# Graph attention on one Trainium2 core: the first stage's edge preparation moved between engines and places

## The chip, the cores and the metric

The kernel runs on one core of one Trainium2 chip. The metric is the device time of one execution in microseconds (us). Engines are called as in the profile: PE (TensorE matmul), PEld (its weight load), DVE (VectorE), ACT (ScalarE), POOL (GpSimd), SP (SyncE, which here only issues transfers).

## What is computed

There are 12,500 nodes with 128 features `x` and 212,500 directed edges, sorted by target `dst`, each with 128 features `edge_attr_128` and one weight. There are 8 heads of 16.

```python
h = relu(layernorm(x))
q = h @ Wq.T + bq ; v = h @ Wv.T + bv          # per node
k = edge_attr_128 @ Wk.T + bk                  # per edge
in_m   = sum(q[src] * k, -1)                   # per edge and head
out_m  = sum(q[dst] * k, -1)
diag_m = sum(q[src] * q[dst], -1)
score  = (segsoftmax(in_m / 4, dst) + segsoftmax(out_m / 4, dst)
          + segsoftmax(diag_m / 4, dst)) * edge_weight1 ** lam
agg = segment_sum(score * v[dst], dst)
out = x + leaky_relu(agg @ Wo.T + bo, 0.1)
```

## The kernel before

The path that runs (`ordered_path`) has a first stage over nodes and a loop over edges.

**First stage.** The nodes lie in 98 tiles of 128, in `xq`. They are loaded in nine parts: tiles 0-3, 4-7, 8-13, 14-27, 28-41, and so on to 84-97. Each part gets statistics on DVE (`statistics`: L817 per tile, then five small sums L822 to L827), and then its scale and shift (`scale`: a square root on ACT L832, a reciprocal L833 and a shift L834 on DVE). 25 groups of four tiles go through a pipeline written out by hand: in step g, ACT rectifies group g + 2 in place (L845), PE turns group g + 1 (L852) and ACT copies it (`hT`, L854), PE multiplies group g by Wq (L860), DVE adds the bias (L863), and SP stores the rows into `q_table` in memory (L864). Then come the scale of a part that is needed four groups on (`ready`), and the statistics of a later part (`measure`).

After that, the dictionary `side` may call a piece of edge preparation in step g. The edge arrays are loaded by POOL as 104 rows of 2048 (`src_r`, `dst_r`, `weight`):

- `edges_1` (step 2) makes the source indices float on DVE (L750) and turns them with 16 PE transposes (L734) and four DVE copies (L735) into `src_i`, the indices of the gathers.
- `edges_2` (step 8) makes the targets float on POOL (L754), subtracts neighbours on DVE (`step`, L756; it takes the buffer of `src_r`), and marks the starts of segments on POOL (L758), stored as term 0 of `fa_d`.
- `edges_3` (step 11) takes each block's base (L763) and subtracts it (L766, four times), on DVE; POOL reorders and casts the result (L769) for `rel_d`.
- `edges_4(c)` (steps 14, 17, 20) splits the weights into three bf16 terms: a POOL copy (L775), a DVE subtraction (L777), and a store of term c + 1 (L743).
- `turn_ws` and `biases` (steps 5, 6) prepare the other weights and biases.

The bf16 results of `edges_2`, `edges_3` and `edges_4` share two buffers (`of`).

After the last group, `gather(0..8)` is issued on POOL, then `fetch_edges(0..5)` (the edge features of six blocks of 512 edges, L644), `fetch(0)` on SP, and `terms_q` (L880 to L889), which splits q into three bf16 terms for `q3_table`.

**Edge loop.** 420 blocks of 512 edges. Each has four indirect gathers of q rows on POOL (L652), issued nine blocks ahead (`LOOK`), and the products, scans and row sums on PE, ACT and DVE.

**Order.** `pin` chains every instruction of an engine in program order. So each engine, SP's queue of transfers too, runs its list in the order of the code, and a waiting instruction holds all behind it.

Of the kernel before, what the change touches and what calls it, by code (L numbers as in the profile page):

```python
# [472 lines left out]
def ordered_path(ctx: ExitStack, tc: tile.TileContext, flag, x, src, dst, edge_attr, edge_weight,  # L473
# [19 lines left out]
    nc = tc.nc  # L493
# [12 lines left out]
    RC = RB * BE  # L506
# [14 lines left out]
    def parts_of(u):  # L521

        return [s for s in range(S)
                if (s == 0 or START * s + RATE - NEAR < UN * (u + 1))
                and (s == S - 1 or UN * u < START * (s + 1) + RATE + NEAR)]
# [59 lines left out]
    LOOK, QQ, AHEAD, EA = 9, 11, 6, 7  # L585
# [6 lines left out]
    def pin(inst):  # L592

        engine = str(inst.ins.engine)
        if engine in pinned:
            tc.add_manual_dep(inst.ins, pinned[engine], mybir.DependencyInfo(
                mybir.DependencyClass.NoSync, mybir.DependencyReason.DATA), reason="in order")
        pinned[engine] = inst.ins.name
        return inst
# [14 lines left out]
    def fetch(t):  # L614

        if t >= T:
            return
        at, part = block_rows(t)
        relb = load.tile([K3, S, BE], BF, name="relb")
        pin(nc.sync.dma_start(relb, rel_d[part].rearrange("(s b) e -> s b e", b=G)  # L620
                              [None, :, at, :].to_broadcast([K3, S, BE])))
        fa = load.tile([4 * S, BE], BF, name="fa", bufs=4)
        for s in range(S):
            pin(nc.sync.dma_start(fa[4 * s:4 * s + 4], fa_d[s * G + t]))
        _, base_v[t] = nc.values_load_multi_w_load_instructions(
            bases[0:1, t, 0:S], engines=[mybir.EngineType.SP], min_val=0, max_val=N - 1,
            skip_runtime_bounds_check_because="the indices of nodes are below N")
        st[t] = dict(relb=relb, fa=fa)
# [8 lines left out]
    def fetch_edges(g):  # L637
        if g < S * T:
            ea = load.tile([P, JN * F], F32, name="ea", bufs=EA)
            b0 = (g % S * G + g // S) * BE  # L640
            n = min(BE, E - b0)
            if n < BE:
                nc.vector.memset(ea, 0.0)
            pin(nc.sync.dma_start(ea[:n // JN, :],  # L644
                                  edge_attr[b0:b0 + n, :].rearrange("(p j) f -> p (j f)", j=JN)))
            eas[g] = ea

    def gather(g):
        if g < S * T:
            qq = gath.tile([P, JN, 2, F], F32, name="qq")  # L650
            for j in range(JN):
                rows = pin(nc.gpsimd.indirect_dma_start(  # L652
                    out=qq[:, j, 0, :], out_offset=None, in_=q_table,
                    in_offset=bass.IndirectOffsetOnAxis(
                        ap=src_i[:, g % S * G + g // S, j:j + 1], axis=0)))
                if (g - LOOK, j) in behind:
                    tc.add_manual_dep(rows.ins, behind[g - LOOK, j], mybir.DependencyInfo(
                        mybir.DependencyClass.Sync, mybir.DependencyReason.SCHED_ONLY),
                        reason="close behind the products")
            qqs[g] = qq  # L660
# [15 lines left out]
    with tc.tile_pool(name="prep", bufs=1) as prep, \  # L676
# [30 lines left out]
        src_r = prep.tile([RW, RC], I32, name="src_r", tag="step")  # L707
# [3 lines left out]
        dst_r = prep.tile([RW, RC + 2], I32, name="dst_r")  # L711
# [5 lines left out]
        weight = prep.tile([RW, RC], F32, name="weight")  # L717
# [11 lines left out]
        def turn_edges(of, to, which=range(RB)):  # L729
            cols = of.rearrange("r (a p j) -> r a j p", a=RB, j=JN)  # L730
            for a in which:
                t_ps = prep_ps.tile([P, JN, RW], F32, name="t_ps")
                for j in range(JN):
                    pin(nc.tensor.transpose(t_ps[:, j, :], cols[:, a, j, :], ident[:RW, :RW]))  # L734
                pin(nc.vector.tensor_copy(to[:, a:NB:RB, :], t_ps.rearrange("p j r -> p r j")))  # L735

        dst_f = dst_r.bitcast(F32)
        src_f = src_r.bitcast(F32)
# [3 lines left out]
        def fa_out(c, of):  # L742
            pin(nc.sync.dma_start(fa_d.rearrange("(r a) c e -> c r a e", a=RB)[c],  # L743
                                  of.rearrange("r (a e) -> r a e", a=RB)))

        def of_tile():
            return prep.tile([P, RC], BF, name="of", bufs=2)[:RW]

        def edges_1():
            pin(nc.vector.tensor_copy(src_f, src_r))  # L750
            turn_edges(src_f, src_i)

        def edges_2():
            pin(nc.gpsimd.tensor_copy(dst_f, dst_r))  # L754
            step = got["step"] = prep.tile([RW, RC + 1], F32, name="step", tag="step")
            pin(nc.vector.tensor_sub(step, dst_f[:, 1:], dst_f[:, :RC + 1]))  # L756
            of = of_tile()
            pin(nc.gpsimd.tensor_scalar(of, step[:, :RC], 0.0, -FAR, op0=ALU.is_gt, op1=ALU.mult))  # L758
            fa_out(0, of)
# [13 lines left out]
        def edges_4(c):  # L773
            of = of_tile()
            pin(nc.gpsimd.tensor_copy(of, weight))  # L775
            if c < 2:
                pin(nc.vector.tensor_sub(weight, weight, of))  # L777
            fa_out(c + 1, of)

        def edges_5(i):  # L780
# [11 lines left out]
        def turn_w(i, to):  # L792
            w_ps = prep_ps.tile([P, F], F32, name="t_ps")
            pin(nc.tensor.transpose(w_ps, w_in[:, i, :], ident))
            pin(nc.scalar.copy(to, w_ps))
# [47 lines left out]
        def rectify(g):  # L843
            for i in tiles_of(g):
                pin(nc.scalar.activation(xq[:, i, :], xq[:, i, :], AF.Relu, bias=shift[:, i:i + 1],  # L845
                                         scale=inv[:, i:i + 1]))

        def turn_h(g):
            n = len(tiles_of(g))
            h_ps = node_ps.tile([P, JN, P], F32, name="h_ps")  # L850
            for b, i in enumerate(tiles_of(g)):
                pin(nc.tensor.transpose(h_ps[:, b, :], xq[:, i, :], ident))  # L852
            hT = hTs[g] = node.tile([P, JN, P], F32, name="hT", bufs=2)
            pin(nc.scalar.copy(hT[:, :n], h_ps[:, :n]))  # L854

        def nodes_q(g):
            n = len(tiles_of(g))
            q_ps = node_ps.tile([P, JN, F], F32, name="q_ps")
            for b in range(n):
                pin(nc.tensor.matmul(q_ps[:, b, :], hTs[g][:, b, :], wq, start=(b == 0),  # L860
                                     stop=(b == n - 1)))
            q = xq[:, g * JN:g * JN + n, :]
            pin(nc.vector.tensor_add(q, q_ps[:, :n], bq_all[:, None, :].to_broadcast([P, n, F])))  # L863
            pin(nc.sync.dma_start(units(q_table, g * 2, n // 2, F),  # L864
                                  q.rearrange("p (u k) f -> p u (k f)", k=2)))
            del hTs[g]
# [3 lines left out]
        def terms_q(g):  # L870
# [11 lines left out]
            if g > 0:  # L882
# [7 lines left out]
                    q3_table[3 * lo:3 * (lo + n * P), :].rearrange("(u p k) f -> p u (k f)", p=P, k=6),  # L890
                    q3.rearrange("p (u k) t f -> p u (k t f)", k=2)))

        side = {2: edges_1, 5: turn_ws, 6: biases, 8: edges_2, 11: edges_3, 14: lambda: edges_4(0),
                17: lambda: edges_4(1), 20: lambda: edges_4(2)}
        turn_w(0, wq)
        parts = [(2 * lo, 2 * hi) for lo, hi in zip(LOADS, LOADS[1:])]

# [2 lines left out]
        def measure(upto):  # L900

            while parts and parts[0][0] < (upto + 1) * JN:
                measured.append(statistics(*parts.pop(0)))

        def ready(upto):

            while measured and measured[0][0] < (upto + 1) * JN:
                scale(*measured.pop(0))
# [3 lines left out]
        for g in range(-2, GN):  # L912
            if g + 2 < GN:
                rectify(g + 2)
            if 0 <= g + 1 < GN:
                turn_h(g + 1)
            if g >= 0:
                nodes_q(g)
            ready(g + 4)
            measure(g + 6 + min(max(g, 0), 6))  # L920
            if g in side:
                side[g]()
        for g in range(LOOK):
            gather(g)
        for g in range(AHEAD):
            fetch_edges(g)
        fetch(0)
        for g in range(GN + 1):
            terms_q(g)
# [142 lines left out]
    with tc.tile_pool(name="work", bufs=2) as work, \  # L1072
# [223 lines left out]
        for g in range(end + 2 * S):  # L1296
# [31 lines left out]
            if g < S:  # L1328
                of = [u for u in range(NU) if g in parts_of(u)]
# [62 lines left out]
```

## Time and profile before

| | |
|---|---|
| median of 3 runs | 2300.62 us (2298.96 to 2305.27) |
| profiled execution: own time, span | 2308.75 us, 2307.0 us |
| busy: PE, PEld, DVE, ACT, POOL | 1816.2, 1395.9, 2148.9, 1515.6, 1666.3 us |
| shares of the span | 79%, 61%, 93%, 66%, 72% |
| moved by DMA | 341.04 MB, 148 GB/s on average |
| mean granted TensorE clock | 0.79 |

The times of instructions come from one profiled execution, whose span starts with its first instruction. A row of the timeline gives the start, the duration, the engine and the line, then output and input with their shapes; "xN" merges N neighbours, and the bracket tells how long the engine had been idle and what released it. A group row gives the total busy time, the mean of one in ns, and the idle time before them. Durations on POOL are rough.

### The profile page before, as it was taken

What the parts mean: (1) busy time and instruction counts of PE and PEld (TensorE: products, weight loads), DVE (VectorE), ACT (ScalarE), POOL (GpSimd) and SP (SyncE); (2) the same over time, 40 slices, a digit from 0 to 9 for tenths busy, and PEclk for the clock granted to TensorE, in tenths of its full rate; (3) what the DMA queues carried; (4) which work ended last, traced back from release to release, by engine and by line L of the source; (5) the groups of instructions that cost most, each with busy time, mean ns of one, the idle gap of its engine ahead of it and who ended that gap; (6) DMA issues with size and microseconds to landing.
All of it is one profiled execution on the core that took longest, in us unless ns stands there. A gap on an engine that the chain in (4) does not pass through costs nothing.

```text
span 2307.0 us, 36031 instructions
## 1 busy us (share of the span) xinstructions
PE 1816.2 (79%) x10629; PEld 1395.9 (61%) x10629; DVE 2148.9 (93%) x2263; ACT 1515.6 (66%) x2797; POOL 1666.3 (72%) x1715
## 2 busy tenths in 40 slices
PE   5458888888878778888777887878788878778876
PEld 4446666666666566666566665666566666556654
DVE  6889999998999999999999999999999999999994
ACT  5667676666676666667666666657666667666772
POOL 3677777777777777777777777777777777777760
PEclk8767777776787797888788778878787788788786
DMA  7785455455454545555544555455555545544531
GB/s 198 242 262 146 144 142 151 135 155 139 129 157 138 149 140 142 154 147 140 156 134 146 145 147 158 136 144 142 152 145 142 153 143 142 158 140 141 142 97 41
DMA packets 306681, 341.04 MB, mean 148 GB/s; under 512 B 137667, under 2 KB 225496, under 8 KB 306165
## 3 DMA queue, kind: packets, MB, share of 16 engines
q1 hardware_dynamic: 244042, 222.69, 32.1%
q0 software_dynamic: 54448, 112.96, 19.3%
q10 hardware_dynamic: 7984, 3.00, 0.5%
q8 instruction: 85, 1.39, 0.2%
q14 instruction: 122, 1.00, 0.1%
HBM read 307.79 MB, written 30.64 MB: 147 GB/s over the span
## 4 chain that ended last, share of the span: by engine, by line
DVE 26%; PE 24%; ACT 16%; issue 16%; DMA 13%; POOL 4%; SPq 1%; DVEq 0%; ACTq 0%; POOLq 0%
DMA qq<-q_table,src_i 10%; PE k_ps L1099 8%; DVE prod L1120 6%; DVE prod L1119 6%; POOL qq L652 4%; PE eT_ps L1089 4%; DVE sum L1180 4%; PE qd_ps L1108 4%; ACT eT L1091 3%; ACT l L1142 3%; ACT relb L1083 3%; PE b_ps L1200 3%; ACT oh L1084 3%; DVE sel L1189 2%; ACT qq L1110 2%
## 5 line engine op out<-in xcount | busy, mean ns | idle before, releaser
L652 POOL DMA_INDIRECT qq<-q_table,src_i x1680 | 1631.5, 971 | 522.9 <-issue 320.6
L1122 DVE TENSOR_REDUCE lT<-prod 128x96 f32<-128x1536 f32 x420 | 736.1, 1753 | 14.4
L1099 PE MATMUL k_ps<-wk,eT 128*128 128x128 f32 x3360 | 603.7, 334 | 66.2 <-ACT eT L1091 58.6
L1099 PEld LDWEIGHTS k_ps<-wk,eT 128*128 128x128 f32 x3360 | 510.3, 232 | 217.0 <-ACT eT L1091 146.1
L1110 ACT COPY qq<-qd_ps 128x512 f32<-128x512 f32 x420 | 245.6, 585 | 578.7 <-PE qd_ps L1108 488.1
L1120 DVE TENSOR_TENSOR prod<-qq,k_ps 128x1024 f32<-128x1024 f32 x420 | 509.4, 1213 | 0.0
L1108 PE MATMUL qd_ps<-win,oh 126*128 126x128 bf16 x1680 | 200.2, 254 | 225.7 <-DVE prod L1119 184.5
L1119 DVE TENSOR_TENSOR prod<-qq,qd_ps 128x512 f32<-128x512 f32 x420 | 284.2, 677 | 66.0 <-ACT qq L1110 37.5
L1089 PE MATMUL eT_ps<-ident,ea 128*128 128x128 f32 x1680 | 332.3, 334 | 12.7 <-DVE found L937 12.7
L1108 PEld LDWEIGHTS <-oh 126*128 126x128 bf16 x1680 | 155.3, 115 | 271.1 <-issue 229.9
L1083 ACT ACTIVATE relb<-relb,before 126x512 bf16<-126x512 bf16 x420 | 306.5, 730 | 0.0
L1091 ACT COPY eT<-eT_ps 128x512 f32<-128x512 f32 x420 | 247.5, 589 | 44.4 <-PE eT_ps L1089 42.3
L1084 ACT ACTIVATE oh<-relb 126x512 bf16<-126x512 bf16 x420 | 264.6, 630 | 17.6 <-DVE flag L960 4.2
L1089 PEld LDWEIGHTS eT_ps<-ident,ea 128*128 128x128 f32 x1680 | 234.8, 176 | 13.0 <-DVE found L937 13.0
L1200 PE MATMUL b_ps<-ident,sum 120*128 120x120 f32 x672 | 147.7, 356 | 91.6 <-ACT l L1142 91.6
L1097 PE MATMUL k_ps<-b,ones 3*128 3x512 bf16 x420 | 191.5, 456 | 10.9 <-DVE prod L1120 9.3
L1213 PE MATMUL w_ps<-back,sel 128*126 128x144 f32 x1344 | 190.1, 295 | 0.6 <-ACT back L1201 0.6
L1200 PEld LDWEIGHTS b_ps<-ident,sum 120*128 120x128 f32 x672 | 104.1, 215 | 138.5 <-ACT l L1142 113.1
L1213 PEld LDWEIGHTS w_ps<-back,sel 128*126 128x126 f32 x1344 | 171.9, 191 | 22.3 <-issue 14.2
L1201 ACT COPY back<-b_ps 128x480 f32<-128x480 f32 x168 | 97.6, 582 | 50.1 <-PE b_ps L1200 50.1
L1152 DVE TENSOR_TENSOR_SCAN u<-l,u,far_ps 120x512 f32<-120x512 f32 x83 | 105.5, 1271 | 0.8 <-ACT l L1142 0.8
L1180 DVE TENSOR_TENSOR_SCAN sum<-keep,sum,up 120x512 f32<-120x512 f32 x83 | 105.9, 1276 | 0.0
(182 smaller groups left out, 1719.1 us busy)
## 6 DMA issues: line engine op xcount, KB each, us to landing
ea<-in_edge_attr_dram SPq DMA_DIRECT2D x419, 256.0 KB
relb<-rel_d SPq DMA_DIRECT2D x84, 630.0 KB
qq<-q_table,src_i POOLq DMA_INDIRECT x1680
win<-q_table SPq DMA_DIRECT2D x420, 31.5 KB
q_table<-q SPq DMA_DIRECT2D x24, 384.0 KB
fa<-fa_d SPq DMA_DIRECT2D x420, 4.0 KB
sums<-rows SPq DMA_DIRECT2D x416, 7.9 KB
q_table<-xq SPq DMA_DIRECT2D x24, 256.0 KB
```

The lines of the kernel that those rows point to most:

```text
L652: rows = pin(nc.gpsimd.indirect_dma_start(out=qq[:, j, 0, :], out_offset=None, in_=q_table, in_offset=bass.IndirectOffsetOnAxis(ap=src_i[: ...
L1083: pin(nc.scalar.activation(d, d, AF.Abs, bias=before[:K3]))
L1084: pin(nc.scalar.activation(oh, d, AF.Relu, bias=1.0, scale=-1.0))
L1089: pin(nc.tensor.transpose(eT_ps[:, j, :], eas[g][:, j * F:(j + 1) * F], ident))
L1091: pin(nc.scalar.copy(eT, eT_ps))
L1099: pin(nc.tensor.matmul(k_ps[:, j, :], eTs[g][:, j, :], wk, start=False, stop=(j == JN - 1)))
L1108: pin(nc.tensor.matmul(qd_ps[:, j, :], ohs[g][:, j * P:(j + 1) * P], d["win"][:, s, :], start=(j == 0), stop=(j == JN - 1)))
L1119: pin(nc.vector.tensor_mul(prod[:, :, 2, :], qqs[g][:, :, 0, :], qds[g]))
L1120: pin(nc.vector.tensor_mul(prod[:, :, 0:2, :], qqs[g], ks[g][:, :, None, :].to_broadcast([P, JN, 2, F])))
L1122: pin(nc.vector.tensor_reduce(lTs[t][:, :, s, :], prod.rearrange("p j i (h d) -> p j (i h) d", d=DIM), AX.X, ALU.add))
L1200: pin(nc.tensor.transpose(b_ps[:, j, :], d["nd"][i][:, j:BE:JN], ident[:R, :R]))
L1213: pin(nc.tensor.matmul(w_ps[:, i].rearrange("p s c -> p (s c)"), d["sel"][:, j, lo:lo + 3, :].rearrange("p s w -> p (s w)"), d["back"][:, ...
```

## The change

Three things are changed, all in the first stage. The cast of the sources goes from DVE to POOL and, with the cast of the targets, into step 0 (`edges_0`); the turning of the sources goes to step 8, and `edges_2` and `edges_3` one step later. The subtraction of neighbours and the two subtractions of weight terms go from DVE to POOL, and the weight terms into steps 1 to 3. The edge features of the six first blocks are issued one block at a time in steps 9 to 14.

```diff
         def edges_1():
-            pin(nc.vector.tensor_copy(src_f, src_r))
             turn_edges(src_f, src_i)
 
+        def edges_0():
+            pin(nc.gpsimd.tensor_copy(src_f, src_r))
+            pin(nc.gpsimd.tensor_copy(dst_f, dst_r))
+
         def edges_2():
-            pin(nc.gpsimd.tensor_copy(dst_f, dst_r))
             step = got["step"] = prep.tile([RW, RC + 1], F32, name="step", tag="step")
-            pin(nc.vector.tensor_sub(step, dst_f[:, 1:], dst_f[:, :RC + 1]))
+            pin(nc.gpsimd.tensor_sub(step, dst_f[:, 1:], dst_f[:, :RC + 1]))
...
             of = of_tile()
             pin(nc.gpsimd.tensor_copy(of, weight))
             if c < 2:
-                pin(nc.vector.tensor_sub(weight, weight, of))
+                pin(nc.gpsimd.tensor_sub(weight, weight, of))
             fa_out(c + 1, of)
...
-        side = {2: edges_1, 5: turn_ws, 6: biases, 8: edges_2, 11: edges_3, 14: lambda: edges_4(0),
-                17: lambda: edges_4(1), 20: lambda: edges_4(2)}
+        side = {0: edges_0, 1: lambda: edges_4(0), 2: lambda: edges_4(1), 3: lambda: edges_4(2),
+                5: turn_ws, 6: biases, 8: edges_1, 9: edges_2, 12: edges_3}
...
             if g in side:
                 side[g]()
+            if 9 <= g < 9 + AHEAD:
+                fetch_edges(g - 9)
         for g in range(LOOK):
             gather(g)
-        for g in range(AHEAD):
-            fetch_edges(g)
         fetch(0)
```

## The prediction

> **What bounds the kernel now.** I read the group table first, then the busy time by stretches, then the timeline of the first stage, then its waits. In the group table and the stretches the reader is to look at POOL (columns of a stretch: PE, PEld, DVE, ACT, POOL busy, then clock, DMA share, GB/s).
>
> ```profile
> L652 POOL DMA_INDIRECT qq<-q_table,src_i x1680 | 1631.5, 971 | 522.9 <-issue 320.6
> 1420.00:1520.00 100.00, 80.33 (x465) 61.33 (x464) 93.42 (x90) 65.89 (x121) 75.89 (x80) 0.77 0.51 145
> ```
>
> Eighty gathers in 100 us are one per 1.25 us: 0.95 busy and a gap of 0.30. In the list of waits no gap of POOL after its first gather is longer than 0.3 us, whatever engine it is put down to. So POOL, whose busy share is lower than that of DVE (93%), never stops in the edge loop, and DVE catches up with it. Hence the span is a sum of three pieces, read from the first and the last gather:
>
> ```profile
> 93.87 7.29 POOL L652 DMA_INDIRECT qq<-q_table,src_i  x1 [10.71 <-DMA ea<-in_edge_attr_dram]
> 2236.62 0.95 POOL L652 DMA_INDIRECT qq<-q_table,src_i  x1 [0.30 <-issue]
> ```
>
> 93.87 before the first gather, 2143.7 of gathers (2237.6 - 93.87), 69.4 of tail (2307.0 - 2237.6). The change touches neither of the last two. What it is worth is how far it moves the first gather, which reads the whole of q_table and so waits for the landing of the last store of L864 (issued at 89.8). The transfer named in the bracket, ea, is only the neighbour in time.
>
> The first stage, in which the change lies (start, duration, engine, line; in brackets the idle time before and its releaser):
>
> ```profile
> 23.25 1.89 POOL L754 CAST dst_r<-dst_r 104x2050 f32<-104x2050 int32 x1 [0.41 <-POOLq L725]
> ...
> 30.91 2.80 DVE L817 BATCH_NORM_STATS2 stats<-xq 128x6 f32<-128x128 f32 x14 [3.48 <-DMA xq<-in_x_dram]
> ...
> 39.94 0.59 ACT L854 COPY hT<-h_ps 128x512 f32<-128x512 f32 x1 [14.15 <-PE h_ps L852]
> ...
> 45.84 5.30 SPq L864 DMA_DIRECT2D q_table<-xq  x7
> ...
> 56.30 2.27 DVE L756 TENSOR_TENSOR step<-dst_r 104x2049 f32<-104x2049 f32 x1
> ...
> 58.67 7.12 POOL L758 TENSOR_SCALAR of<-step 104x2048 bf16<-104x2048 f32 x1 [33.52 <-DVE step L756]
> ...
> 61.91 1.32 DVE L822 TENSOR_TENSOR sums<-stats 128x14 f32<-128x14 f32 x1
> 63.16 0.17 DVE L823 TENSOR_TENSOR sums<-stats 128x14 f32<-128x14 f32 x1
> ...
> 65.22 0.60 DVE L763 COPY base_c<-dst_r 104x4 f32<-104x4 f32 x1
> ...
> 67.66 3.94 POOL L769 CAST of<-dst_r 104x2048 bf16<-104x2048 f32 x1 [1.88 <-DVE dst_r L766]
> ...
> 69.96 1.68 DVE L834 SCALAR_TENSOR_TENSOR shift<-sums,inv 128x14 f32<-128x14 f32 x1
> ...
> 71.54 1.90 POOL L775 CAST of<-weight 104x2048 bf16<-104x2048 f32 x1
> ```
>
> Two things are to be seen. ACT stands still for 14.15 us, because PE holds the turning of the sources (behind DVE's copy of L750, which is behind the late load of x). [...] L834, usually 0.17, takes 1.68 and ends with POOL's L769 (71.60); L822, usually 0.18, takes 1.32 until 4.5 us after L758's start; the copy of L763 ends with L758 (65.8). From 70 to 80 ACT is busy 10.00 of 10 us: from there ACT sets the pace to the last store.
>
> [...] no POOL instruction with two inputs is in this trace. [...]
>
> **The change, part by part.**
>
> Removed from DVE: L750 (1.23), L756 (2.27), two L777 (4.58): 8.1 us. L750 also goes from in front of the transposes, so PE and ACT run on at 25.8 instead of waiting to 39.9. But activation group 7 then needs the shift of tiles 28 to 41, which on DVE stands behind the statistics of the part of x that lands at 30.91: 30.91 + 2.8 + five sums 0.65 + L863 0.69 + reciprocal and shift 0.4 = 35.5, against 42.98 now. At best 7.4 us are won here.
>
> Turning the sources: the 16 transposes and four copies, 35.7 to 39.7 now, come behind group 8, where DVE is the late engine: 2.6 us of DVE, and PE waits for its buffers.
>
> Added to POOL: the sources' cast, a cast like L754 (1.9), and three subtractions. Each is bounded below by the one-input row (1.9) and above by L758 (7.1)[...]. POOL's new order from 23.25: two casts to 27.05, term copy (L775, 1.9) to 28.95, subtraction to 33.5, copy to 35.4, subtraction to about 40. The third copy waits for a buffer of two, which the store of the first term frees; SP issues that only after bases and tops and two stores (45.84 + 1.5), and such stores land 4.5 to 5.5 us after issue (71.62 to 76.10, 75.72 to 81.27): about 52. So the copy ends near 54, the step subtraction near 58.5, L758 near 65.6: **as late as now** (65.8). The base copy of L763, the rebased edges, L769 and the shift behind it hang on that end, as before, so most of the 7.4 us is given back even if nothing else is held.
>
> What is held: each statistics part has five two-input sums and a shift. For tiles 28 to 41 the first sum is due at 26.14, in POOL's run to 40. L834 shows the hand-over: it ran as L769 ended and POOL's next instruction began at once (71.54). If each hand-over lets one DVE instruction through, the five sums end with the casts and subtractions at 27.05, 28.95, 33.5, 35.4 and 40.0. Behind them on DVE are queued L863 of group 2, the next statistics and their sums, L863 of group 3 and the shift: 0.7 + 2.8 + 0.65 + 0.7 + 0.5 = 5.35, so group 7 starts at 45.4 instead of 42.98. DVE then has two parts of statistics (6.9), five additions (3.3), biases (1.83), a shift (0.4), the sources' copies (2.6): 60.4. Only then is the buffer free (step takes src_r's) for POOL's step subtraction, to about 64.4, L758 to 71.5. The shift that group 14 needs passes after 68.9 and L863: 70.5 (64.73 now). L763 goes at 71.5, L766 (1.67) to 73.6, L769 to 77.6, and the shift behind it at 77.6 against 71.64: **+6.0**.
>
> Edge features: six issues of 0.5 us leave the stretch 90.63 to 93.64 on SP, where no gather waits for them, and stand between stores. Their 1.57 MB (6 x 256 KB) at the 271 GB/s of 88 to 90 are 5.8 us of transfer ahead of the last stores; term stores of 3 x 0.43 MB (4.7 us) leave that stretch in exchange: **+1.1**. The queue freed at 90 helps fetch and the q3 stores; DVE starts its edge loop earlier, POOL does not, so that is worth nothing. If POOL's lead went, it would count.
>
> Sum for the likeliest case: +7.1, first gather at 101, span 2314.1 for the profiled execution of 2307.0 (own time 2308.75, 8.1 above the median). Against the median of 2300.62: **2307.7, say 2308**.
>
> **The rivals.**
>
> *DVE passes in bursts.* At a hand-over all sums that are ready go through, as L823 to L827 did at 63.16. Then group 7 starts at 36.5 to 41.7, POOL's run ends at 65.6 to 68.7, the late shift comes at 71.6 to 74.6 (71.64 now): 0 to +3, with the transfers up to +4: 2301 to 2305. For it: that burst[...].
>
> *The holds are short.* DVE gets through, POOL waits: group 7 at 35.5, so ACT is idle about 6.5 us there (from 29) and, as an estimate, 6.5 more while PE turns the sources behind a late DVE: 13 instead of 19.8 (14.15, and 5.64 before group 14). Subtractions nearer 2 us would also let L758 end at 60. Then -6.8 to -8: 2293 to 2294. It decides if group 7 starts before 37 and group 14 before 58. Against it: 1.68 at L834.
>
> *Long subtractions.* At 7.1 instead of 4.5, two in the first run and one in the second: 3 x 2.6 = 7.8 more: 2315.
>
> *The change does not do what it says* would be POOL's late work delaying the first gather itself: not seen, since its last cast ends at 71 to 78.
>
> **How the numbers follow.** 0.3% is 6.9 us, about what a measurement of this kernel can tell from no change. One by one (with the long subtractions) 0.58, centre 2308: its sum lies at the bound and its unknown prices mostly add, so 0.45 beyond it and 0.13 within. Bursts 0.18, within. Short holds 0.24, of which 0.22 beyond. Slower 0.45, same 0.33, faster 0.22. The likeliest case's own range is 2304 to 2316; the range that takes in the short holds is 2292 to 2316.
>
> **What would show it.** POOL's subtractions near 4.5 us between 29 and 40; DVE sums and shifts of 1 to 4 us there, where 0.17 is usual; group 7 (rectify of tiles 28 on) at 41 to 46; L758 ending at 66 to 72; no wait of 14 us of hT; the first gather at 95 to 101, and gathers still 1.25 us apart. Wrong, if the first gather starts before 92, or if it stays and the span moves: then POOL is not the bound.

## The result and the profile after

The changed kernel takes 2323.95 us (median of 4 runs, 2320.10 to 2325.52) against 2301.33 us for the kernel before (4 runs, 2298.96 to 2305.27): a ratio of 1.0091, 95% interval 1.0076 to 1.0105. It is **slower by 22.6 us**. The prediction had the sign and not the size: 2308, with a range that ended at 2316. The profiled execution after took 2322.66 us, with a span of 2320.9.

From L755 of the kernel before on, lines carry numbers that are 2 higher: the subtraction L756 is L758 now, and what was L758 is L760; L864 is L866, L881 and L887 are L883 and L889.

The group of gathers in the page of the changed kernel, and the same 100 us of the edge loop (PE, PEld, DVE, ACT, POOL busy, then clock, DMA share, GB/s):

```profile
L652 POOL DMA_INDIRECT qq<-q_table,src_i x1680 | 1642.7, 978 | 532.3 <-issue 321.7
1420.00:1520.00 100.00, 80.71 (x503) 63.17 (x502) 97.98 (x94) 69.00 (x128) 75.91 (x80) 0.85 0.53 149
```

In the stretch there are again 80 gathers in 100 us, so the loop's pace is what it was. The group's total is 11.2 us higher, though the same 1680 gathers are issued.

The first stage after, from the timeline (start, duration, engine, line; in brackets the idle time before and its releaser):

```profile
22.88 1.89 POOL L753 CAST src_r<-src_r 104x2048 f32<-104x2048 int32 x1
...
29.94 4.06 POOL L779 TENSOR_TENSOR weight<-weight,of 104x2048 f32<-104x2048 f32 x1
30.01 4.01 DVE L827 SCALAR_TENSOR_TENSOR sums<-sums 128x14 f32<-128x14 f32 x1
...
41.66 1.65 ACT L847 ACTIVATE xq<-xq,shift,inv 128x128 f32<-128x128 f32 x4 [5.08 <-DVE shift L836]
...
52.67 1.96 POOL L777 CAST of<-weight 104x2048 bf16<-104x2048 f32 x1 [12.54 <-DMA fa_d<-of]
...
58.53 3.60 POOL L758 TENSOR_TENSOR step<-dst_r 104x2049 f32<-104x2049 f32 x1 [3.90 <-PE t_ps L734]
...
59.33 0.58 ACT L856 COPY hT<-h_ps 128x512 f32<-128x512 f32 x1 [6.77 <-PE h_ps L854]
...
62.23 7.12 POOL L760 TENSOR_SCALAR of<-step 104x2048 bf16<-104x2048 f32 x1
...
68.30 1.65 ACT L847 ACTIVATE xq<-xq,shift,inv 128x128 f32<-128x128 f32 x4 [3.61 <-DVE shift L836]
```

The stage went much as the rival "bursts" had it: ACT's wait of 14.15 us is gone, and four of 8.15, 5.08, 6.77 and 3.61 us stand for the 14.15 and 5.64 of before. The first gather starts at 95.68, 1.8 us later than before. That is not 22.6 us. The rest stands in the next rows of SP, POOL and DVE:

```profile
95.66 33.70 SPq L891 DMA_DIRECT2D q_table<-q  x25
95.68 1.10 POOL L652 DMA_INDIRECT qq<-q_table,src_i  x1 [20.36 <-DMA fa<-fa_d]
95.73 2.28 DVE L787 TENSOR_REDUCE bad<-step 104x1 f32<-104x2048 f32 x1
97.08 11.18 POOL L652 DMA_INDIRECT qq<-q_table,src_i  x1 [0.30 <-issue]
97.93 0.68 DVE L883 TENSOR_TENSOR xq<-xq,q 128x512 f32<-128x512 f32 x1
98.53 0.68 DVE L889 TENSOR_TENSOR q<-xq,q 128x512 bf16<-128x512 f32 x1
...
101.54 2.29 DVE L789 SCALAR_TENSOR_TENSOR step<-step,dst_r 104x2048 f32<-104x2048 f32 x1
...
107.35 0.58 DVE L735 COPY ends<-t_ps 128x416 f32<-128x416 f32 x1
...
108.57 3.79 POOL L652 DMA_INDIRECT qq<-q_table,src_i  x1 [0.30 <-issue]
...
111.46 0.58 DVE L735 COPY ends<-t_ps 128x416 f32<-128x416 f32 x1
...
112.66 3.80 POOL L652 DMA_INDIRECT qq<-q_table,src_i  x1 [0.30 <-issue]
...
116.77 3.81 POOL L652 DMA_INDIRECT qq<-q_table,src_i  x1 [0.30 <-issue]
...
120.88 8.69 POOL L652 DMA_INDIRECT qq<-q_table,src_i  x1 [0.30 <-issue]
...
129.87 1.33 POOL L652 DMA_INDIRECT qq<-q_table,src_i  x1 [0.30 <-issue]
```

A gather's usual duration is 0.95. The first six take 32.37 us here; before they took 12.91 (7.29, 0.97, 0.95, 1.46, 0.95, 1.29). So the seventh starts at 129.87 instead of 108.60: 1.81 of later start and 19.46 of slower gathers, **21.27 us**. The 51st gather is still 20.2 us late (185.93 against 165.74). From there on both kernels issue one gather per 1.27 us on average (1.271 before, 1.267 after), and nothing gives the loss back at once.

These two executions themselves differ by less than the medians: 2322.66 against 2308.75, or 13.9 us, because the profiled execution of before lies 7.4 us above its median and that of after 1.3 below. The difference shows in the edge loop: the 1674 gathers after the first six took 8.3 us less in the execution after (so the group's total rose by 11.2 and not by 19.46), and the last gather comes 12.7 us later than before (2249.34 against 2236.62). That the other executions lose about 21 us in their first gathers too is inferred; one more execution of the changed kernel, shown below, does.

What the slow gathers share is seen in the same rows. From 97.93 to 128.7 DVE is never idle: it runs the subtractions of `terms_q`, L883 and L889 in turn, 0.68 long, one per 0.60, two SBUF inputs each, and among them only L789 and four copies L735. Each of the five held gathers here ended 0.89 to 0.91 us after the start of a DVE instruction of another kind: at 108.26, 0.91 after the copy of L735 from PSUM began; at 112.36, 116.46 and 120.58, 0.90, 0.89 and 0.90 after the next three copies; at 129.57, 0.89 after the reduction L939. The first gather, which starts 0.05 before the one-input reduction of L787, took only 1.10.

The edge loop of the same executions shows the same contrast. After 250 us 42 gathers of the changed kernel take more than 1.2 us (1.77 at most). All 42 start while DVE runs L1191 (38 of 49 that start there) or L1157 (4 of 42): two instructions that read two tensors in SBUF (`ends` and `places`; `u` and `l`). The 574 that start beside L1121 or L1122, whose second input is in PSUM, and the 488 that start beside the one-input reduction L1124 take 0.96 at most. In the kernel before, all 49 such gathers start beside an instruction with two inputs in SBUF.

And in the kernel before there was a hole:

```profile
98.06 32.09 SPq L889 DMA_DIRECT2D q_table<-q  x25
...
101.47 0.97 POOL L652 DMA_INDIRECT qq<-q_table,src_i  x1 [0.30 <-issue]
102.69 0.62 ACT L880 CAST q<-xq 128x512 bf16<-128x512 f32 x1 [5.83 <-DMA q_table<-q]
102.74 0.95 POOL L652 DMA_INDIRECT qq<-q_table,src_i  x1 [0.30 <-issue]
...
103.34 0.69 DVE L881 TENSOR_TENSOR xq<-xq,q 128x512 f32<-128x512 f32 x1 [3.13 <-ACT q L880]
```

SP reached the first store of `q3` only at 98.06, behind edge features and `fa`. The buffers of `q3` came free late, ACT waited 5.83 us for one, and DVE stood still for 3.13 us, from 100.21. The first gather, 7.29 us long, ended at 101.16, 0.95 into that hole. After it the others came in at once. In the changed kernel SP begins these stores at 95.66, 3.1 us after DVE's first L883, and nobody runs out of buffers.

### The profile page after: what moved, and what is told of

The parts are those of the page before. It is cut to its first block, busy times and chain, and to the rows that moved or that the text cites. A ratio compares the mean times of both kernels' runs of the same rounds, so it can differ in the third digit from the quotient of the medians.

```text
span 2320.9 us, 36037 instructions
## 1 busy us (share of the span) xinstructions
PE 1809.4 (78%) x10629; PEld 1396.5 (60%) x10629; DVE 2151.0 (93%) x2259; ACT 1513.5 (65%) x2797; POOL 1691.2 (73%) x1719
## 4 chain that ended last, share of the span: by engine, by line
PE 26%; DVE 23%; ACT 17%; issue 14%; DMA 13%; POOL 4%; SPq 1%; DVEq 0%; ACTq 0%; POOLq 0%
DMA qq<-q_table,src_i 10%; PE k_ps L1101 8%; DVE prod L1121 5%; DVE prod L1122 5%; PE eT_ps L1091 4%; POOL qq L652 4%; DVE sum L1182 4%; PE qd_ps L1110 4%; ACT eT L1093 3%; ACT relb L1085 3%; ACT l L1144 3%; ACT oh L1086 3%; PE b_ps L1202 3%; DVE sel L1191 2%; ACT qq L1112 2%
## 5 line engine op out<-in xcount | busy, mean ns | idle before, releaser
L652 POOL DMA_INDIRECT qq<-q_table,src_i x1680 | 1642.7, 978 | 532.3 <-issue 321.7
L1124 DVE TENSOR_REDUCE lT<-prod 128x96 f32<-128x1536 f32 x420 | 736.2, 1753 | 14.4
L1122 DVE TENSOR_TENSOR prod<-qq,k_ps 128x1024 f32<-128x1024 f32 x420 | 509.6, 1213 | 0.0
L1121 DVE TENSOR_TENSOR prod<-qq,qd_ps 128x512 f32<-128x512 f32 x420 | 284.4, 677 | 77.1 <-ACT qq L1112 39.7
L1091 PEld LDWEIGHTS eT_ps<-ident,ea 128*128 128x128 f32 x1680 | 233.0, 175 | 12.7 <-DVE found L939 12.7
```

Of the source, the lines that this page charges most:

```text
L652: rows = pin(nc.gpsimd.indirect_dma_start(out=qq[:, j, 0, :], out_offset=None, in_=q_table, in_offset=bass.IndirectOffsetOnAxis(ap=src_i[: ...
L1091: pin(nc.tensor.transpose(eT_ps[:, j, :], eas[g][:, j * F:(j + 1) * F], ident))
L1121: pin(nc.vector.tensor_mul(prod[:, :, 2, :], qqs[g][:, :, 0, :], qds[g]))
L1122: pin(nc.vector.tensor_mul(prod[:, :, 0:2, :], qqs[g], ks[g][:, :, None, :].to_broadcast([P, JN, 2, F])))
L1124: pin(nc.vector.tensor_reduce(lTs[t][:, :, s, :], prod.rearrange("p j i (h d) -> p j (i h) d", d=DIM), AX.X, ALU.add))
```

## The theories

**A.** DVE's unbroken run of subtractions with two SBUF inputs holds POOL's gathers; the change took away the pause in which they used to come in. **B.** The transfers hold them: the stores of `q3`, now earlier, fill the queues. **C.** The subtractions on POOL leave the engines in an order in which gathers are slow.

For B there is little in the trace: between 100 and 125 the DMA share (the busy share of the transfer engines) is 0.72 to 0.87 after and 0.94 to 0.99 before, lower where the gathers are slower.

The experiments ran on three chips on which this kernel is slower, called the first, second and third test chip below. The kernel before takes 2902.39, 2922.75 and 2918.26 us there, at a granted clock of 0.71 to 0.73. POOL also waits in the edge loop there: in the changed kernel it is idle for 1107.3 us before its gathers, where it was 532.3 above (for PE, `b_ps`, 195.7 of it, longest 5.5). Why the loop is that much slower there is not known. So each ratio is against the kernel before on the same chip, and totals that an expectation puts near 2300 do not apply.

The main reading is the start of the seventh gather. The first gather of the changed kernel with or without fillers starts at 92.7 on the second test chip and at 95.7 to 96.4 elsewhere, so shifts of a few us between chips are not read; the time from the first gather to the seventh does not depend on them.

## Experiments: the parts of the change

**The edge features back behind the gathers**, all else as changed:

```diff
-            if 9 <= g < 9 + AHEAD:
-                fetch_edges(g - 9)
         for g in range(LOOK):
             gather(g)
+        for g in range(AHEAD):
+            fetch_edges(g)
```

> The changed kernel with the six first blocks of edge features issued behind the gathers again, as before; all else as changed. Theory A (DVE's unbroken run of subtractions with two SBUF inputs holds the first gathers, and before it was broken because SP came late to the q3 stores, so ACT and DVE had to pause for a q3 buffer): the pause of about 3 us comes back, at most one gather is long (6 to 10 us), gather 7 starts at 108 to 112 us instead of 129.9, time 2303 to 2308. Theory B (the q3 stores, which start 2.4 us earlier, fill the transfer queues and the gathers wait for room): the stores are late again, so also 2303 to 2308. Theory C (the POOL subtractions leave POOL or the buffers in a state that makes its first gathers slow): unchanged, 2322 to 2326.

2901.08 us, ratio 0.9993 (0.9972 to 1.0013). From its timeline:

```profile
92.58 2.28 DVE L787 TENSOR_REDUCE bad<-step 104x1 f32<-104x2048 f32 x1
92.70 8.93 POOL L652 DMA_INDIRECT qq<-q_table,src_i  x1 [20.55 <-DMA ea<-in_edge_attr_dram]
...
101.87 0.69 DVE L883 TENSOR_TENSOR xq<-xq,q 128x512 f32<-128x512 f32 x1 [1.21 <-ACT q L882]
...
109.25 0.94 POOL L652 DMA_INDIRECT qq<-q_table,src_i  x1 [0.30 <-issue]
```

SP's first store of `q3` comes at 96.69, 7.3 us after DVE's run began, and DVE pauses for 1.21 us before 101.87 (about 3 was expected). The first gather ends at 101.63, in that pause, and the seventh starts at 109.25, nearly as early as in the kernel before. So the edge features' place is needed for the loss. A and B expected the same here; C, which had the gathers slow, is contradicted.

**The edge features alone moved**, in the kernel before:

```diff
+            if 9 <= g < 9 + AHEAD:
+                fetch_edges(g - 9)
         for g in range(LOOK):
             gather(g)
-        for g in range(AHEAD):
-            fetch_edges(g)
```

> The kernel before with one edit: the six first blocks of edge features issued one at a time in steps 9 to 14. Theories A and B: the slow first gathers appear without any of the POOL work; gather 7 at 120 to 130 us instead of 108.6, time 2312 to 2322. Theory C: no slow gathers, 2299 to 2303.

2899.53 us, ratio 0.9992 (0.9974 to 1.0010). Slow gathers were expected and did not come: the longest of the first seven takes 3.86 us, and the seventh starts at 105.09. SP's queue suggests why:

```profile
85.93 0.85 SPq L743 DMA_DIRECT2D fa_d<-of  x1
86.87 4.34 SPq L864 DMA_DIRECT2D q_table<-xq  x4
91.26 0.68 SPq L620 DMA_DIRECT2D relb<-rel_d  x1
...
100.18 0.69 DVE L881 TENSOR_TENSOR xq<-xq,q 128x512 f32<-128x512 f32 x1 [2.84 <-ACT q L880]
```

The last weight term is still stored at 85.93, late, with four stores of `q_table` behind it. SP begins the stores of `q3` at 94.07, 8.0 us after DVE's run began at 86.07, and DVE pauses for 2.84 us. So the early edge features alone do not take the pause away. As this queue reads, it has two causes that stand in for one another, late weight terms and late edge features, and the change moves both away; a kernel with early weight terms alone was not run. Together with the next two kernels:

| kernel | DVE's run begins | SP's first `q3` store | later by | pause of DVE | seventh gather | first to seventh |
|---|---|---|---|---|---|---|
| before | 88.95 | 98.06 | 9.1 | 3.13 | 108.60 | 14.73 |
| edge features alone moved | 86.07 | 94.07 | 8.0 | 2.84 | 105.09 | 10.66 |
| edge features back | 89.40 | 96.69 | 7.3 | 1.21 | 109.25 | 16.55 |
| changed | 92.56 | 95.66 | 3.1 | none | 129.87 | 34.19 |
| changed, second test chip | 89.60 | 92.71 | 3.1 | none | 126.93 | 34.21 |
| changed, subtractions on DVE | 94.38 | 97.49 | 3.1 | none | 132.73 | 35.07 |

**The changed kernel itself**, on the second test chip:

> The changed kernel itself, beside the kernels with fillers on the same chip. A (DVE's unbroken run of subtractions with two SBUF inputs holds the gathers): on this chip too the first gather is short (about 1.1) and the next five take 3 to 11 us each, so that the seventh starts at 125 to 131. On a chip where the edge loop is bound by POOL the total is 1.008 to 1.0105 of the kernel before; on one where it is not, the late gathers are paid from the lead of nine blocks and the total is within 0.3%. B (the transfers hold them): the same here, but then the fillers change nothing.

2939.45 us, ratio 1.0060 (1.0042 to 1.0078). The gathers take 1.11, 11.19, 3.79, 3.81, 3.81 and 8.69 us, nearly the figures of the comparison above. Neither of the two expected totals came: 16.7 us of loss are left of some 20, less than where POOL alone bounds the loop and more than the 0.3% that was expected where it waits elsewhere too.

**The three subtractions back on DVE**, all else as changed:

```diff
-            pin(nc.gpsimd.tensor_sub(step, dst_f[:, 1:], dst_f[:, :RC + 1]))
+            pin(nc.vector.tensor_sub(step, dst_f[:, 1:], dst_f[:, :RC + 1]))
...
-                pin(nc.gpsimd.tensor_sub(weight, weight, of))
+                pin(nc.vector.tensor_sub(weight, weight, of))
```

> The changed kernel with its three POOL subtractions returned to DVE (L758 and both L779), all else as changed. A: they end 20 us before the first gather and have no part in the slow gathers; DVE's run is as unbroken as in the changed kernel, so the gathers are slow again and the seventh starts at 118 to 131. The first gather may start anywhere from 88 to 97. C (the subtractions on POOL leave DVE or POOL in a state, or an order, in which the gathers are slow): the seventh gather starts by 110, and the total is at most 1.003 of the kernel before where POOL bounds the edge loop.

2942.92 us, ratio 1.0065 (1.0040 to 1.0089).

```profile
97.56 2.28 DVE L787 TENSOR_REDUCE bad<-step 104x1 f32<-104x2048 f32 x1
97.66 12.55 POOL L652 DMA_INDIRECT qq<-q_table,src_i  x1 [20.52 <-DMA fa<-fa_d]
110.51 3.69 POOL L652 DMA_INDIRECT qq<-q_table,src_i  x1 [0.30 <-issue]
...
122.71 8.36 POOL L652 DMA_INDIRECT qq<-q_table,src_i  x1 [0.30 <-issue]
```

The gathers are as slow without any subtraction on POOL, and the seventh starts at 132.73 (1.7 beyond the span that was named, since the first one is late). **C falls.**

## Experiments: the run of subtractions

**A filler behind each pair**, in the changed kernel: a memset of 128x64, which reads nothing and takes 0.11 us, so that DVE issues something else than a two-input subtraction once per block of `terms_q`. No transfer and no wait is changed.

```diff
+        idle = prep.tile([P, 64], F32, name="idle")
...
                 pin(nc.vector.tensor_sub(q3[:, :, 2, :], q, q3[:, :, 1, :]))
+                pin(nc.vector.memset(idle, 0.0))
```

> The changed kernel with a memset of 128x64 on DVE (no input, about 0.1 us) behind each second subtraction of terms_q, so that the run of two-input subtractions has an opening every 1.3 us; 24 memsets, about 2.4 us of DVE. Theory A: a gather gets through at each opening, none is longer than about 2 us, gather 7 at 104 to 107, time 2299 to 2304. Theory B: transfers are as before the edit, gathers stay at 3.8 to 11 us, 2322 to 2328.

2894.00 us, ratio 0.9974 (0.9952 to 0.9995), on the first test chip.

```profile
95.84 1.10 POOL L652 DMA_INDIRECT qq<-q_table,src_i  x1 [20.37 <-DMA fa<-fa_d]
97.25 2.98 POOL L652 DMA_INDIRECT qq<-q_table,src_i  x1 [0.30 <-issue]
...
103.03 3.10 POOL L652 DMA_INDIRECT qq<-q_table,src_i  x1 [0.30 <-issue]
...
105.28 0.11 DVE L891 MEMSET idle<- 128x64 f32 x1
...
107.69 0.95 POOL L652 DMA_INDIRECT qq<-q_table,src_i  x1 [0.30 <-issue]
```

The first gather is where it was, and the seventh starts at 107.69 instead of 129.87, 11.85 us after the first. Two gathers take about 3 us, where 2 at most was expected. The one of 3.10 starts beside L789, a single instruction of 2.25 us with two SBUF inputs; it outlasts L789 by 2 us and ends at 106.13, 0.85 after the next memset began. This contradicts B: the same stores go out in the same order, SP begins them at 95.82 (95.66 before the edit), and the gathers pass.

Beside the unfilled kernel, on the second test chip:

> The changed kernel with a 0.11 us memset on DVE after each L889. A: the seventh gather starts at 103 to 110 instead of 129.87, and where POOL bounds the edge loop the total falls by what the seventh gather gains: 2324 - 21 = 2303, a ratio of 1.000 to 1.003. B: 2320 or more, a ratio above 1.007. Where POOL does not bound it: 0.995 to 1.000 under both.

2919.24 us, ratio 0.9998 (0.9973 to 1.0024), against 1.0060 without the fillers: 20.2 us less, for 25 memsets. The two intervals do not meet. The seventh gather starts at 104.54 instead of 126.93. And once more on the third test chip:

> The changed kernel with the 0.11 us memset behind each L889, as before, beside the next two. A: the seventh gather at 103 to 110; a total within 0.3% of the kernel before. B: a total above 1.006.

2918.88 us, ratio 1.0004 (0.9987 to 1.0021), the seventh gather at 108.28.

**One hole**: the changed kernel with seven memsets of 128x420, once, behind L789, where the kernel before had its pause.

```diff
             if g % 3 == 2:
                 edges_5(g // 3)
+            if g == 5:
+                for _ in range(7):
+                    pin(nc.vector.memset(idle, 0.0))
```

> The changed kernel with one hole in DVE's run: seven memsets of 128x420 (about 2.5 us together) once, behind L789, where the kernel before had its pause of 3.13 us. A with lock (once a gather has come in, the next ones come in at the borders of DVE's operations): the held gather ends in the hole, the following ones take 0.95 to 1.5 each, the seventh starts at 107 to 113, and where the total of the changed kernel is 1.006 or 1.009 of the kernel before, this one is within 0.3% of it. A without lock (each gather needs a hole or a copy from PSUM of its own): two gathers pass in the hole, then again one per 4.1 us, the seventh at 116 to 122, and most of the loss stays. B (transfers): no change, seventh at 125 or later.

2920.05 us, ratio 1.0003 (0.9981 to 1.0026).

```profile
97.06 7.57 POOL L652 DMA_INDIRECT qq<-q_table,src_i  x1 [0.30 <-issue]
...
103.83 0.41 DVE L937 MEMSET idle<- 128x420 f32 x1
...
104.93 0.94 POOL L652 DMA_INDIRECT qq<-q_table,src_i  x1 [0.30 <-issue]
106.18 0.95 POOL L652 DMA_INDIRECT qq<-q_table,src_i  x1 [0.30 <-issue]
107.44 1.54 POOL L652 DMA_INDIRECT qq<-q_table,src_i  x1 [0.30 <-issue]
107.53 0.63 DVE L884 TENSOR_TENSOR xq<-xq,q 128x512 f32<-128x512 f32 x1
...
109.28 0.94 POOL L652 DMA_INDIRECT qq<-q_table,src_i  x1 [0.30 <-issue]
110.53 0.94 POOL L652 DMA_INDIRECT qq<-q_table,src_i  x1 [0.30 <-issue]
...
111.77 1.40 POOL L652 DMA_INDIRECT qq<-q_table,src_i  x1 [0.30 <-issue]
```

The held gather ends at 104.63, 0.80 after the first memset began. From 107.53 DVE runs its subtractions again as densely as before, and yet the gathers now pass in 0.94 to 1.54 each; the seventh starts at 110.53, 14.87 us after the first (34.2 in the changed kernel, 14.73 in the kernel before). **One hole repairs nearly the whole loss.** So A needs its second half: the gather that stood behind the run was held (7.57), and once it had ended in the hole, the five behind it took 0.94 to 1.54 each beside the memsets and the same run of subtractions.

What decides between the two phases is not settled, and two simple answers fail. It is not the distance to the last subtraction: 0.12 us after one a gather is held in the changed kernel (108.57 after 108.45: 3.79), 0.09 us after one a gather passes here (111.77 after 111.68: 1.40), and with the subtractions on DVE one that starts 0.23 us after (110.51 after 110.28) takes 3.69. And it is not only the kind of instruction that runs when the gather starts. With the edge features back, and with the subtractions on DVE, the first gather starts 0.12 and 0.10 us after the one-input reduction L787 and is not let in during its remaining 2.2 us; it takes 8.93 and 12.55. In the edge loop of the changed kernel the 488 gathers beside the reduction L1124 took 0.96 at most.

## A version that might beat both

In the kernel before, too, the first gather is held (7.29). **The fillers in the kernel before**, the same edit:

> The kernel before with the same memsets. Theory A: its one long gather (7.29 us, which ended 0.95 us after DVE's run of subtractions paused at 100.2) shrinks to under 2 us, so 5 to 6 us are won: 2294 to 2297. Theory B: the first gather stays long, 2300 to 2304.

2893.94 us, ratio 0.9971 (0.9955 to 0.9988); the first gather takes 2.75 (under 2 was expected), the seventh starts at 103.05. On the second test chip:

> The kernel before with the same memsets. A: the first gather is shorter than its 7.29 us, the seventh starts at 102 to 106 instead of 108.60, and where POOL bounds the edge loop the total is 3 to 6 us shorter: 2295 to 2298, a ratio of 0.9975 to 0.9985, below the kernel before and the changed one. B: 2299 to 2303.

2922.96 us, ratio 0.9992 (0.9973 to 1.0011); the seventh at 104.31. On the third test chip:

> The kernel before with the memsets. A: the seventh gather at 102 to 106; the total 0.9970 to 0.9995 of the kernel before, the lower end where POOL bounds the edge loop. B: 1.000.

2914.78 us, ratio 0.9991 (0.9970 to 1.0012); the seventh at 104.35. From the first gather to the seventh it is 11.82, 11.38 and 11.77 us, about 3 less than the 14.73 of the kernel before; the rest of the earlier start is an earlier first gather (91.23 to 92.93 against 93.87). The total follows in one of three comparisons; on chips where POOL is not alone in setting the pace, a gain of this size is at the edge of what is measured. At the pace of the first comparison this version was not measured, so whether it beats the kernel before there is open.

**The fillers, and of the change the cast of the sources alone**:

```diff
         def edges_1():
-            pin(nc.vector.tensor_copy(src_f, src_r))
+            pin(nc.gpsimd.tensor_copy(src_f, src_r))
```

> The kernel before with the memsets and with the cast of the sources (L750) on POOL instead of DVE, its place and that of the turning unchanged; POOL's cast runs at 23 to 25 instead of DVE's at 34.4. The wait of 14.15 us of hT shrinks to 2 to 7, the activation of group 7 starts at 36 to 38 instead of 42.98, and the first gather at 86 to 91. Total 4 to 7 us below the kernel before with memsets alone, where the gathers' chain decides (0.994 to 0.998 of the kernel before). Rival: DVE's four copies L735 push the statistics of the part that lands at 30.91 back, and the shift that group 14 needs stays behind L758 and L769 as it was: then the first gather stays at 91 to 94 and the total that of the memsets alone.

2917.29 us, ratio 0.9995 (0.9974 to 1.0016).

```profile
26.79 1.10 PE L734 MATMUL t_ps<-ident,src_r 104*128 104x104 f32 x8
35.38 1.66 PE L734 MATMUL t_ps<-ident,src_r 104*128 104x104 f32 x8 [7.48 <-DVE src_i L735]
...
37.93 0.58 ACT L854 COPY hT<-h_ps 128x512 f32<-128x512 f32 x1 [9.57 <-PE h_ps L852]
```

The wait of hT only falls from 14.15 to 9.57. PE turns the first half of the sources at once, by 27.9, and then waits 7.48 us for DVE to empty its buffers: the copies of L735 stand on DVE behind the statistics of the part of x that lands at 30.5 (L817, 30.52 to 33.32, and its sums to 34.04) and begin at 34.73. So with the cast gone, the late part of x holds the turning at step 2. Group 7 starts at 40.79, where 36 to 38 was expected. The first gather starts at 90.37, 2.2 earlier than with fillers alone on this chip (92.58), and the total does not show it. This is neither the gain that was expected (86 to 91 for the gather is met, the total is not) nor the rival, which had the gather where it was.

## Why the prediction was wrong

**What held.** The end of L760, with the bases behind it, within the cases (65.6 to 71.5 predicted, 69.35 measured, 65.8 before); the third copy behind its buffer's store (54 predicted, 52.67 to 54.63 measured); short DVE instructions held through POOL's run (L827 4.01 where 0.17 is usual). Of the cases for the first stage, "bursts" is the one that came: group 7 starts at 41.66 (predicted 36.5 to 41.7, against 45.4 for one by one), and the first gather is 1.8 us later (predicted 0 to +3). The likeliest case, +7.1, was wrong in that step: at the hand-over at 29.85 three sums passed in place of one, and at 40.1, where POOL's run ended, all that were left.

**Sizes and readings.** POOL's subtractions took 4.06, 4.06 and 3.60 us; the prediction counts each at 4.5, a length between its bounds of 1.9 and 7.1 that the trace of before does not show: 1.8 us too much over three. The edge features' transfer, +1.1, does not show: ACT's last hT ends 3.6 us later than before (90.89, 87.28) and the first gather starts only 1.8 later, so the stretch between them became 1.8 us shorter. In the sum, 60.4 and 4.5 make 64.9, not 64.4. And of the DVE instructions that the prediction names as long beside POOL, L834 (1.68) and L822 (1.32) read two SBUF tensors, the copy of L763 (0.60) one.

**The step that failed** is in the sentence on the bound: "93.87 before the first gather, 2143.7 of gathers, 69.4 of tail. The change touches neither of the last two." From it followed, under edge features, that a queue of SP freed at 90 "is worth nothing" because "DVE starts its edge loop earlier, POOL does not". In fact the freed queue let ACT and DVE run `terms_q` without a pause, and this run held POOL: +19.46 us within the first six gathers. The sum with the two measured terms is +1.81 + 19.46 = +21.3, against +22.6 of the medians. The rival that was to end at 2315 named long subtractions; what came was another mechanism.

**The sign was luck.** The kernel was to be slower because its first gather would come 7.1 us later. It came 1.8 later, and by the prediction's own measure (6.9 us) that alone would have been no change. The kernel is slower for a reason that the prediction put at nothing.

The evidence was in a line that the prediction shows: the first gather with 7.29 us, beside a usual 0.95. It was read for its start alone. The prediction looked for DVE instructions that are long beside POOL's arithmetic (L834, 1.68 where 0.17 is usual) and not for gathers that are long beside DVE's work. The slow gathers of the edge loop, all beside two-input instructions (42 of more than 1.2 us after, 49 before), and the 11.18 beside the run agree with A; the two gathers held from within the reduction L787 (8.93 and 12.55) are not explained by it.

**The signs.** Of those that were to show the prediction right, nearly all came (no wait of 14 us, group 7 at 41.66, the first gather at 95.68), and one failed: "gathers still 1.25 us apart" does not hold from the second gather to the seventh. The sign of being wrong was a first gather that stays while the span moves, "then POOL is not the bound". Something near it came (1.8 and 13.9 us), and yet POOL is still the bound: the first gathers themselves had become longer.

## What to carry to other kernels

A row whose duration is eight times the usual one can be a stall inside the instruction, as the first gather's 7.29 us was against 0.95: no waiting time in the brackets shows it, so compare each first or single instance with the mean of its group. When an engine is freed or a queue shortened, ask which pauses it was causing, and who used them: here a late store queue gave DVE a pause of 3 us that POOL lived on. Where POOL issues the indirect transfers that set the pace, it is worth trying to break a long run of two-input DVE work beside them with an instruction that doesn't read two SBUF tensors; 25 memsets of 0.11 us were worth 20 us here.

## What the runs showed of the hardware

- A run of two-input DVE subtractions (0.68 us each, one per 0.60) held an indirect gather of POOL for up to 12.55 us, the first 2.2 of them beside the reduction L787, and not for one instruction. In the changed kernel held gathers ended 0.89 to 0.91 us after the start of a copy from PSUM (L735, every 4.1 us); with fillers, 0.85 and 0.87 after that of a memset of 0.11 us; in the kernel before, 0.95 into a pause of DVE.
- In the edge loop of the changed kernel every gather of more than 1.2 us (42, after 250 us) started beside a DVE instruction with two SBUF inputs; beside the reduction L1124 (488) and beside products with one input in PSUM (574) they took 0.96 at most.
- After one stretch of about 3.7 us with memsets alone (103.83 to 107.53) the gathers passed the same run of subtractions in 0.94 to 1.54 us each; without it four of them took 3.79 to 8.69.
- POOL's f32 subtraction over 104x2048 took 4.06 us where one input is bf16 (L779) and 3.60 us where both are f32 (L758); a DVE instruction of a usual 0.17 us (L827) that started 0.07 us after such a start took 4.01.
